# Layer 3 attention: full-width products as four column tiles of 32, and one copy of a pair of transposes on VectorE

## The chip, the cores and the metric

The kernel runs on one core of a Trainium2 chip. The metric is the device time of one execution in microseconds, as the median of three runs. Beside it stands one profiled execution, from which every duration below comes.

## The reference, cut to what matters

The program is a network of four mixed layers on an input of 8 images with 256 channels and 32 x 32 positions, all in 32-bit floats. The change touches only the attention of layer 3. There, every image is 1024 tokens of 256 channels, in 8 heads of 32 channels:

```
qkv = x @ qkv_w.T + qkv_b
scores = einsum('bnhd,bmhd->bhnm', q, k) * scale          # scale = 32 ** -0.5
t = square(scores + 5.0)
attn = t / sum(t, axis=-1)
out = einsum('bhnm,bmhd->bnhd', attn, v) @ proj_w.T + proj_b
```

The input x is the layer-normed state, and the result is added to the state. After it comes a mixture of experts with a router. The denominators have a closed form: the sum over m of (scale q.k + 5) squared needs only the second moments of k per head (a 32 x 32 block) and the sum of k, both independent of the query.

## The kernel before, in words

P is 128, N is 1024 tokens, C is 256 channels, so KC = 2 chunks of 128 channels, HF = 512 is half of the tokens and NT = 8 is the number of token tiles of 128. A chunk of 128 channels holds four heads of 32.

The attention of layer 3 is the generator `fast3`, and its main loop is `attention`. The loop has 256 steps, numbered from 0: 8 images x 2 halves of the queries x 2 chunks x 8 tiles of keys, so 32 steps for an image (image 2 has steps 64 to 95). One step i does, in this order:

- scores (L2745): four matmuls, one for each head of the chunk. A head has 32 channels, so each uses 32 rows of the array and all 128 columns ("32*128" in the profile). They fill two PSUM tiles s from a pool of three.
- squares (L2751): two ScalarE activations of 128 x 1024, giving the tile e of the step. ScalarE works in program order.
- `run(i, beside)`: pieces of other streams that are due at this step: the norm of the image after next (`norm`, on VectorE by L1030 to L1041, plus two short activations), the routing of the image before (`routed`, L2435 is its costliest VectorE line), a fetch, and now and then sorting. What they issue goes to VectorE, ScalarE, GpSimd and the DMA queues.
- a small piece, if one is due and the stream of pieces stands at number 12, 14 or 26 (`SMALL`), so that this step holds two pieces.
- values of step i - 1 (L2725): four matmuls, one for each head, with 128 rows and 32 columns each ("128*32"), accumulated in the single PSUM tile A over 8 key tiles. At the end of such a row VectorE multiplies A by the reciprocal denominators into o (L2730), and A is free again.
- one piece: the output projection of an earlier half (`project`, L2709, two for each half), or else the next piece of the next image's `products`.

The pieces of `products(b + 1)`, 30 for an image, are in order: 8 of k and q (label qk), 4 of v, 4 of kT (two pairs of transposes of k, numbers 12 to 15), 2 of G (moments of k, 129 columns wide, L2668), 4 of Gq (moments times q, L2680), 4 of D (sums over the channels of a head, L2688), then 4 of xn (transposes of the image after that, numbers 26 to 29). All have 128 rows and 128 columns ("128*128"). Each takes the one PSUM bank X and ends with one instruction that empties it: ScalarE for q, k, kT, D and xn, VectorE for v, G, Gq and proj. A D piece gives ScalarE a logarithm (L2689), and every second one an exponential over 1024 columns (L2691).

The profile shows a product of 32-bit floats as two matmul instructions, each with a weight load (PEld); a transpose is one. Matmuls through the helper `linear` all bear line L78, so they are told apart by the tile names. Inside the loop the order on TensorE, VectorE and ScalarE is that in which the code issues the instructions (`net.in_order`); for all else a scheduler arranges them. Before the loop, image 0's products are issued all at once, together with image 1's transposes.

Of the kernel before, what the change touches and what calls it, by code (L numbers as in the profile page):

```python
# [17 lines left out]
P = 128  # L18
B = 8
C = 256  # L20
KC = C // P
N = 1024
HF = 512
# [874 lines left out]
class Fast:  # L898
# [114 lines left out]
    def token_norm_steps(self, dst, x, pool, placed=True):  # L1013

        n = x.shape[1]
        r = pool.tile([P, 2, n], F32, tag="tn_r", name="tn_r")
        yield from self.token_statistics(r, x, pool, placed)
        for t in range(n):
            self.nc.vector.tensor_scalar(
                dst[:, t, :], x[:, t, :], r[:, 0, t : t + 1], r[:, 1, t : t + 1], ALU.mult, ALU.add  # L1020
            )

    def token_norm_pieces(self, dst, x, pool):

# [1532 lines left out]
def fast3(net, io):  # L2557
    tc, nc = net.tc, net.nc
    NH = 4
    NT = N // P  # L2560
    SCALE = 32 ** (-0.5)
    with ExitStack() as ctx, ExitStack() as tok, ExitStack() as att, ExitStack() as bef:
# [10 lines left out]
        wq, wkk, wv = (net.load(wp, f"l3_w{n}", "(k p) o -> p k o", p=P) for n in "qkv")  # L2573
        wo = net.load(wp, "l3_wo", "(k p) o -> p k o", p=P, eng=nc.scalar)
# [5 lines left out]
        heads = net.load(wp, "f3_heads")  # L2580
# [10 lines left out]
        ps = bank("bo")  # L2591
# [10 lines left out]
        xs, xts, xns, qs, ks, vs, rs = ({} for _ in range(7))  # L2602
# [8 lines left out]
        def norm(b):  # L2611
# [8 lines left out]
            yield from net.token_norm_pieces(normed, xs[b], norms)  # L2620
            nc.gpsimd.tensor_tensor(xs[b], xs[b], bo.unsqueeze(1).to_broadcast([P, NT, C]), ALU.add)

        def turned(b, h, c):
            if b not in xns:
                pool, tag = (own["k1"], "xn") if own else (xpool, "x2")
                xns[b] = pool.tile([P, KC, N], F32, tag=tag, name="xn")
            ps = bank("xn")
            for t in range(4):
                nc.tensor.transpose(ps[:, bass.ts(t, P)], xts[b][:, 4 * h + t, bass.ts(c, P)], net.ident)
            nc.scalar.copy(xns[b][:, c, bass.ts(h, HF)], ps)  # L2630

        def projections(b):

            xn = xns.pop(b)
            for d, w, bias, name in ((ks, wkk, bk, "k"), (qs, wq, bq, "q")):
                d[b] = own["two"].tile([P, KC, N], F32, tag=name, name=name)
                for c in range(KC):
                    for h in range(2):
                        ps = bank("qk")
                        net.linear(ps, w, xn, bass.ts(c, P), bass.ts(h, HF))  # L2640
                        nc.scalar.activation(d[b][:, c, bass.ts(h, HF)], ps, AF.Identity, bias=bias(c))
                        yield
            v = vs[b] = own["two"].tile([P, NT, C], F32, tag="v", name="v")
            for t2 in range(0, NT, 2):
                ps = bank("v")
                for i in range(2):
                    net.linear(ps[:, bass.ts(i, C)], xn, wv, bass.ts(t2 + i, P), slice(0, C))
                nc.vector.tensor_copy(v[:, t2 : t2 + 2].rearrange("p t c -> p (t c)"), ps)
                yield

        def denominators(b):

            kt = flat("kt").rearrange("p (t c n) -> p t c n", c=KC, n=P + 4)
            nc.gpsimd.memset(kt[:, :, :, P], 1.0)
            for t2 in range(0, NT, 2):
                ps = bank("kT")
                for i in range(2):
                    for c in range(KC):
                        nc.tensor.transpose(
                            ps[:, i * C + c * P : i * C + (c + 1) * P], ks[b][:, c, bass.ts(t2 + i, P)], net.ident  # L2660
                        )
                nc.scalar.copy(kt[:, t2 : t2 + 2, :, :P], ps.rearrange("p (h c n) -> p h c n", c=KC, n=P))
                yield
            gm = own["k2"].tile([P, KC, P + 4], F32, tag="gm", name="gm")
            for c in range(KC):
                G = bank("G")
                for t in range(NT):
                    nc.tensor.matmul(  # L2668
                        G[:, : P + 1], lhsT=kt[:, t, c, :P], rhs=kt[:, t, c, : P + 1],
                        start=(t == 0), stop=(t == NT - 1),  # L2670
                    )
                nc.vector.tensor_tensor(gm[:, c, : P + 1], G[:, : P + 1], heads[:, 0].to_broadcast([P, P + 1]), ALU.mult)
                yield
            prod = own["k1"].tile([P, KC, N], F32, tag="prod", name="prod")
            r = rs[b] = own["two"].tile([P, KC, N], F32, tag="r", name="r")

            def product(c, h):
                ps = bank("Gq")
                cols = bass.ts(h, HF)
                nc.tensor.matmul(ps, lhsT=gm[:, c, :P], rhs=qs[b][:, c, cols], start=True, stop=True)  # L2680
                nc.vector.scalar_tensor_tensor(
                    prod[:, c, cols], ps, gm[:, c, P : P + 1], qs[b][:, c, cols], ALU.add, ALU.mult
                )

            def weights(c, h):
                ps = bank("D")
                cols = bass.ts(h, HF)
                nc.tensor.matmul(ps, lhsT=heads[:, 0, :P], rhs=prod[:, c, cols], start=True, stop=True)  # L2688
                nc.scalar.activation(r[:, c, cols], ps, AF.Ln, scale=SCALE * SCALE, bias=rest)  # L2689
                if h:  # L2690
                    nc.scalar.activation(r[:, c, :], r[:, c, :], AF.Exp, scale=-1.0)  # L2691
                    nc.sync.dma_start(out=net.sums3[8 * b + 4 * c : 8 * b + 4 * c + 4, :], in_=r[0:P:32, c, :])

            both = [(c, h) for c in range(KC) for h in range(2)]
            for c, h in both:
                product(c, h)
                yield
            for c, h in both:
                weights(c, h)
                yield  # L2700

        def attention(beside, parts):

            steps = [(b, hh, c, kt) for b in range(B) for hh in range(2) for c in range(KC) for kt in range(NT)]
            es, os, accs, projects = {}, {}, {}, []

            def project(b, hh, t2):
                ps = bank("proj")
                for t in range(2):  # L2709
                    net.linear(ps[:, bass.ts(t, C)], os[b], wo, bass.ts(4 * hh + t2 + t, P), slice(0, C))  # L2710
                xh = xs[b][:, 4 * hh + t2 : 4 * hh + t2 + 2].rearrange("p t c -> p (t c)")
                nc.vector.tensor_tensor(xh, ps, xh, ALU.add)

# [20 lines left out]
            def piece():  # L2734
                if next(parts[0][2], "over") == "over":
                    parts.pop(0)
                    if not parts or parts[0][0] > i:
                        return
                    next(parts[0][2])
                parts[0][1] += 1  # L2740

            for i, (b, hh, c, kt) in enumerate(steps):
                ss = [own["S"].tile([P, 2, HF], F32, tag="S", name="s") for _ in range(2)]
                for h in LATEST:
                    nc.tensor.matmul(  # L2745
                        ss[h // 2][:, h % 2], lhsT=ks[b][32 * h : 32 * h + 32, c, bass.ts(kt, P)],
                        rhs=qs[b][32 * h : 32 * h + 32, c, bass.ts(hh, HF)], start=True, stop=True,
                    )
                e = es[i] = own["e"].tile([P, NH, HF], F32, tag="e", name="e")
                for j in range(2):  # L2750
                    anchor[:] = [nc.scalar.activation(e[:, 2 * j : 2 * j + 2], ss[j], AF.Square, scale=SCALE, bias=five)]  # L2751
                run(i, beside)
                turn = bool(projects) and projects[0][0] <= i
                if not turn and parts and parts[0][0] <= i and parts[0][1] in SMALL:
                    piece()
                if i:
                    values(i - 1)
                if projects and projects[0][0] <= i:
                    project(*projects.pop(0)[1:])
                elif parts and parts[0][0] <= i:  # L2760
                    piece()
# [3 lines left out]

        LATEST = (2, 3, 0, 1)
        SMALL = (12, 14, 26)
        STEPS, anchor = 4 * NT, []

        def products(b):  # L2770

# [32 lines left out]
        for _ in projections(0):  # L2804
            pass
# [5 lines left out]
        beside, parts = [], []  # L2811
# [16 lines left out]
        def run(i, streams):  # L2828

            while streams:  # L2830
                d = min(streams, key=lambda d: d[0])
                if d[0] > i:
                    break
                try:
                    next(d[2])
                    d[0] += d[1]
                except StopIteration:
                    streams.remove(d)
# [511 lines left out]
```

## Time and profile before

| what | time |
|---|---|
| median of three runs | 4171.65 us (4161.88 to 4172.53) |
| profiled execution, its own time | 4110.1 us |
| profiled execution, span from first to last instruction | 4108.3 us |
| loop of layer 3's attention within the span | 2804 to 3720 us |
| TensorE busy in the loop | 887.72 of 916.00 us |
| VectorE / ScalarE busy in the loop | 475.25 / 645.24 us |
| a step with scores and values alone, at its shortest | 2.07 us |
| a step with a q or k piece / a v piece | 3.98 / 3.99 us |
| a step with a Gq or D piece / with G | 3.12 / 4.05 us |
| a step with two kT pieces | 4.50 us |

A line of a timeline gives the start in us, the length in us, the engine, the line of the code, the operation, the tiles (out, then in), the part of the array (rows * columns) and the count. The length runs until the last of the merged instructions has ended, so it overlaps the next one. To know what a block costs TensorE, take the difference of two starts. A line of waits gives who waited for whom, the us in total, how often, and the longest.

### The profile page before, as it was taken

Reading aid. Unit: us, or ns where it says so; the run is one execution under the profiler, and the core shown is the slowest. Engines: PE = TensorE matmul, PEld = TensorE weight load, DVE = VectorE, ACT = ScalarE, POOL = GpSimd, SP = SyncE. Lnnn points to the kernel's source line nnn. Section 1 sums busy time; section 2 is a strip of 40 time slices with the busy share of each in tenths; the row PEclk is TensorE's granted clock in tenths of the full one; section 3 lists DMA queues with packets and bytes.
Section 4 is the critical chain, followed back from the end, with each engine's and each line's share of the span. In section 5 each row is a group of like instructions: output and inputs, shape, how many; then the busy total and the mean of one; then the engine's idle time right before and its main releaser. Section 6 shows DMA issues by size and latency. Waiting matters only on the chain. (4 is left out here: it accounts for less than half of the span.)

```text
span 4108.3 us, 52125 instructions
## 1 busy us (share of the span) xinstructions
PE 3745.4 (91%) x19046; PEld 1810.0 (44%) x19046; DVE 2510.4 (61%) x5010; ACT 2306.0 (56%) x3142; POOL 569.1 (14%) x646
## 2 busy tenths in 40 slices
PE   8999999999978788789999978989999999999997
PEld 3323333333334444444444435654333333336886
DVE  2398798798896489952322255852355665467455
ACT  4556566566554377743333445535776766776454
POOL 0000000000000000000000012441000051035753
PEclk9999999999998899989999988999999999999998
DMA  3313223323221577720000012432320041046676
GB/s 102 115 44 111 102 69 115 103 69 106 79 93 55 175 250 291 266 101 11 31 21 21 27 55 90 144 128 65 108 99 25 32 137 50 22 137 192 207 237 218
DMA packets 209947, 442.19 MB, mean 108 GB/s; under 512 B 22025, under 2 KB 132572, under 8 KB 197140
## 3 DMA queue, kind: packets, MB, share of 16 engines
q1 hardware_dynamic: 186580, 387.21, 28.5%
q0 software_dynamic: 19440, 46.45, 3.4%
q10 hardware_dynamic: 3664, 5.11, 0.4%
q8 instruction: 154, 2.52, 0.3%
q14 instruction: 109, 0.89, 0.1%
HBM read 283.34 MB, written 162.28 MB: 108 GB/s over the span
## 5 line engine op out<-in xcount | busy, mean ns | idle before, releaser
L1286 DVE SCALAR_TENSOR_TENSOR a<-hp,w_f_vec,a 128x961 f32<-128x961 f32 (+1 forms) x496 | 608.4, 1232 | 100.0 <-ACT a L1279 91.3
L2751 ACT ACTIVATE e<-s,five 128x1024 f32<-128x1024 f32 x512 | 542.2, 1110 | 217.4 <-PE s L2745 216.2
L2745 PE MATMUL s<-q,k 32*128 32x512 f32 x2048 | 306.1, 641 | 0.0
L1438 ACT ACTIVATE e<-s 128x1024 f32<-128x1024 f32 x256 | 250.2, 1023 | 72.2 <-PE s L1432 61.5
L1392 DVE TENSOR_TENSOR sum<-sum,e 128x1024 f32<-128x1024 f32 x192 | 230.4, 1219 | 86.8 <-ACT e L1438 86.8
L2725 PE MATMUL A<-e,v 128*32 128x512 f32 x2048 | 274.5, 608 | 4.7 <-DVE o L2730 3.4
L1396 PE MATMUL A<-e,va 128*32 128x512 f32 x2048 | 264.1, 615 | 0.0
L2435 DVE SCALAR_TENSOR_TENSOR junk<-mo_x,w_f_wr 128x256 f32<-128x256 f32 x512 | 250.2, 489 | 13.3
L78 PE MATMUL pi<-xn,w_l_wpi 128*128 128x512 f32 x512 | 240.6, 611 | 14.7 <-ACT u L1539 9.2
L1432 PE MATMUL s<-q,k 32*128 32x512 f32 x1024 | 179.9, 649 | 2.5 <-ACT e L1438 2.5
L2950 PE MATMUL h<-xk,w 128*128 128x128 f32 x1192 | 153.8, 284 | 11.6 <-DVE xk L2936 11.5
L1743 PE MATMUL acc<-wt,z 128*64 128x192 f32 (+4 forms) x1344 | 123.5, 326 | 44.2 <-DVE wt L1798 43.9
L1048 POOL DMA_INDIRECT res<-y,to x149 | 149.6, 1004 | 102.7 <-DVE y L2974 41.6
L2919 ACT COPY w<-w_l3f_w 128x512 f32 x149 | 92.4, 626 | 122.0 <-PE h L2950 118.7
L78 PEld LDWEIGHTS pi<-xn,w_l_wpi 128*128 128x128 f32 x512 | 93.8, 193 | 151.0 <-issue 112.5
L2950 PEld LDWEIGHTS h<-xk,w 128*128 128x128 f32 x1192 | 150.8, 200 | 17.6 <-DVE xk L2936 14.0
L1048 POOL DMA_INDIRECT so<-xl,rows x128 | 130.7, 1021 | 192.1 <-issue 151.1
L2745 PEld LDWEIGHTS s<-q,k 32*128 32x128 f32 x2048 | 91.0, 183 | 147.1 <-issue 142.2
L1477 ACT ACTIVATE hp<-pi,pib 128x512 f32<-128x512 f32 x128 | 87.2, 690 | 114.9 <-PE pi L78 114.9
L2970 PE MATMUL y<-w_l3f_w,hid 128*128 x596 | 145.5, 385 | 4.4 <-ACT hid L2956 2.5
L1347 POOL MEMSET thrice<- 32x128 f32 x32 | 6.3, 196 | 1013.8 <-PE pe L1363 1013.7
L1396 PEld LDWEIGHTS A<-e,va 128*32 128x32 f32 x2048 | 58.2, 111 | 174.5 <-issue 173.1
(404 smaller groups left out, 7032.9 us busy)
## 6 DMA issues: line engine op xcount, KB each, us to landing
row<-shifts SPq DMA_DIRECT2D x144, 512.0 KB
x<-d SPq DMA_DIRECT2D x31, 1024.0 KB
xs<-so SPq DMA_DIRECT2D x73, 260.0 KB
so<-zero SPq DMA_DIRECT2D x5, 3380.0 KB
thrice<-vimg SPq DMA_DIRECT2D x64, 256.0 KB
gated<-st SPq DMA_DIRECT2D x32, 512.0 KB
hc<-gated SPq DMA_DIRECT2D x32, 512.0 KB
xl<-mox SPq DMA_DIRECT2D x64, 256.0 KB
```

Of the source, the lines that this page charges most:

```text
L78: self.nc.tensor.matmul(ps, lhsT=w[:, i, m], rhs=src[:, i, cols], start=(i == 0), stop=(i == k - 1))
L1048: made = self.nc.gpsimd.indirect_dma_start(**args)
L1286: nc.vector.scalar_tensor_tensor(to, fr, taps(t_), to, ALU.mult, ALU.add)
L1392: nc.vector.tensor_tensor(half, half, e[j], ALU.add)
L1396: nc.tensor.matmul(state["A"][32 * h : 32 * h + 32, c, :], lhsT=vas[b][:, kt, c, 32 * h : 32 * h + 32], rhs=e[h // 2][:, h % 2, :], start= ...
L1432: nc.tensor.matmul(ss[h // 2][:, h % 2], lhsT=ks[b][32 * h : 32 * h + 32, bass.ts(kt, P)], rhs=qs[b][32 * h : 32 * h + 32, bass.ts(gq, HF) ...
L1438: nc.scalar.activation(es[i][j], ss[j], AF.Exp, scale=SCALE)
L2435: nc.vector.scalar_tensor_tensor(junk, xn[:, t, :], 1.0, self.wr[:, e, :], ALU.mult, ALU.mult, accum_out=pr[:, t, e : e + 1])
L2725: nc.tensor.matmul(A[32 * h : 32 * h + 32], lhsT=vs[b][:, kt, c * P + 32 * h : c * P + 32 * h + 32], rhs=e[:, h, :], start=first, stop=last,)
L2745: nc.tensor.matmul(ss[h // 2][:, h % 2], lhsT=ks[b][32 * h : 32 * h + 32, c, bass.ts(kt, P)], rhs=qs[b][32 * h : 32 * h + 32, c, bass.ts(h ...
L2751: anchor[:] = [nc.scalar.activation(e[:, 2 * j : 2 * j + 2], ss[j], AF.Square, scale=SCALE, bias=five)]
L2950: nc.tensor.matmul(ps[:, j, m], lhsT=ws[j][:, k, bass.ts(m, P)], rhs=xk[:, j, k], start=(k == 0), stop=(k == KC - 1),)
```

## The change

Products with 128 weight columns are issued as four matmuls of 32 columns each: to PSUM partitions 0 to 31, 32 to 63 and so on, all with the same moving operand. That is the form which the values already have. It concerns q, k, v, G, Gq, D and proj, in the loop and before it; the transposes stay as they are. Second, a small piece (the first of two in a step) moves ahead of `run(i, beside)`, and while it is issued the list `quick` is filled, which sends its copy to VectorE instead of ScalarE. The second piece of the step copies on ScalarE as before.

```diff
+    def columns(self, ps, lhsT, rhs, **flags):
+        for h in range(P // 32):
+            self.nc.tensor.matmul(ps[32 * h : 32 * h + 32], lhsT=lhsT[:, 32 * h : 32 * h + 32], rhs=rhs, **flags)
+
+    def linear_columns(self, ps, w, src, m, cols, k=KC):
+        for i in range(k):
+            self.columns(ps, w[:, i, m], src[:, i, cols], start=(i == 0), stop=(i == k - 1))
...
+        def copy(dst, src):
+            (nc.vector.tensor_copy if quick else nc.scalar.copy)(dst, src)
+
...
-            nc.scalar.copy(xns[b][:, c, bass.ts(h, HF)], ps)
+            copy(xns[b][:, c, bass.ts(h, HF)], ps)
...
-                        net.linear(ps, w, xn, bass.ts(c, P), bass.ts(h, HF))
+                        net.linear_columns(ps, w, xn, bass.ts(c, P), bass.ts(h, HF))
...
-                    net.linear(ps[:, bass.ts(i, C)], xn, wv, bass.ts(t2 + i, P), slice(0, C))
+                    net.linear_columns(ps[:, bass.ts(i, C)], xn, wv, bass.ts(t2 + i, P), slice(0, C))
...
-                nc.scalar.copy(kt[:, t2 : t2 + 2, :, :P], ps.rearrange("p (h c n) -> p h c n", c=KC, n=P))
+                copy(kt[:, t2 : t2 + 2, :, :P], ps.rearrange("p (h c n) -> p h c n", c=KC, n=P))
...
-                    nc.tensor.matmul(
-                        G[:, : P + 1], lhsT=kt[:, t, c, :P], rhs=kt[:, t, c, : P + 1],
-                        start=(t == 0), stop=(t == NT - 1),
+                    net.columns(
+                        G[:, : P + 1], kt[:, t, c, :P], kt[:, t, c, : P + 1], start=(t == 0), stop=(t == NT - 1)
                     )
...
-                nc.tensor.matmul(ps, lhsT=gm[:, c, :P], rhs=qs[b][:, c, cols], start=True, stop=True)
+                net.columns(ps, gm[:, c, :P], qs[b][:, c, cols], start=True, stop=True)
...
-                nc.tensor.matmul(ps, lhsT=heads[:, 0, :P], rhs=prod[:, c, cols], start=True, stop=True)
+                net.columns(ps, heads[:, 0, :P], prod[:, c, cols], start=True, stop=True)
...
-                    net.linear(ps[:, bass.ts(t, C)], os[b], wo, bass.ts(4 * hh + t2 + t, P), slice(0, C))
+                    net.linear_columns(ps[:, bass.ts(t, C)], os[b], wo, bass.ts(4 * hh + t2 + t, P), slice(0, C))
...
-                run(i, beside)
                 turn = bool(projects) and projects[0][0] <= i
                 if not turn and parts and parts[0][0] <= i and parts[0][1] in SMALL:
+                    quick.append(i)
                     piece()
+                    quick.clear()
+                run(i, beside)
                 if i:
                     values(i - 1)
...
-        STEPS, anchor = 4 * NT, []
+        STEPS, anchor, quick = 4 * NT, [], []
```

## The prediction

> **What bounds the kernel now.** I read the busy shares first, then the busy time by stage, then the timeline of single steps, then TensorE's waits in the stage that the change touches.
>
> ```profile
> PE 3745.4 (91%) x19046; PEld 1810.0 (44%) x19046; DVE 2510.4 (61%) x5010; ACT 2306.0 (56%) x3142; POOL 569.1 (14%) x646
> ```
> ```profile
> 2804.00:3720.00 916.00, 887.72 (x5351) 321.33 (x5349) 475.25 (x1702) 645.24 (x699) 167.06 (x159) 1.00 0.24 76
> ```
> The second line (stage and its length; busy PE, PEld, DVE, ACT, POOL; clock; DMA) is the loop of layer 3's attention: PE is busy 887.72 of 916 us, DVE half, ACT 70%. So PE's own work is the bound there; but "busy" holds gaps between instructions, and those the timeline shows.
>
> ```profile
> 3040.30 1.14 PE L2745 MATMUL s<-q,k 32*128 32x512 f32 x8
> 3041.37 1.07 PE L2725 MATMUL A<-e,v 128*32 128x512 f32 x8
> 3042.37 1.13 PE L2745 MATMUL s<-q,k 32*128 32x512 f32 x6
> ```
> ```profile
> 3082.55 1.14 PE L2745 MATMUL s<-q,k 32*128 32x512 f32 x8
> 3083.62 1.07 PE L2725 MATMUL A<-e,v 128*32 128x512 f32 x8
> 3084.62 1.99 PE L78 MATMUL v<-w_l_wv,xn 128*128 128x256 f32 x8
> 3086.54 1.14 PE L2745 MATMUL s<-q,k 32*128 32x512 f32 x8
> ```
> ```profile
> 145.15 1.92 PE L1396 MATMUL A<-e,va 128*32 128x512 f32 x16
> 147.00 0.70 PE L1432 MATMUL s<-q,k 32*128 32x512 f32 x2
> ```
> Read differences of starts. Scores take 1.07, values 1.00 to the next start; the v piece takes 1.92 for 8 full-width instructions. Steady full-width work of that shape ran 47 instructions in 10.31 us (y, L2248); less the last one's 0.38 that is 9.93 / 46 = 0.216 each, and 8 x 0.216 = 1.73. The other 0.19 to 0.20 is paid for entering and leaving a full-width block. The q/k piece says the same: 1.92 for four, while h (L78) ran 15 in 6.60 us, (6.60 - 0.59) / 14 = 0.43 each, 1.72. Layer 0 has column tiles in a row: 16 instructions, four rounds of four tiles, take 1.85 to the next start; two rounds take 1.00 above. A further round of four column tiles thus costs 0.43, what one full-width instruction over the same 512 columns costs.
>
> The stalls are at pairs of transposes:
>
> ```profile
> 3099.59 0.66 PE L2659 MATMUL kT<-ident,k 128*128 128x128 f32 x4
> 3101.79 0.59 ACT L2662 COPY kt<-kT 128x512 f32<-128x512 f32 x1
> 3102.43 0.66 PE L2659 MATMUL kT<-ident,k 128*128 128x128 f32 x4 [1.19 <-ACT kt L2662]
> ...
> 3105.81 0.69 DVE L2730 TENSOR_TENSOR o<-A,r 128x512 f32<-128x512 f32 x1
> ```
> ```profile
> PE kT L2659 <- ACT kt L2662: 16.7, 14, 1.2
> PE xn L2629 <- ACT xn L2630: 5.3, 6, 1.7
> PE A L2725 <- DVE o L2730: 3.4, 1, 3.4
> ```
> The second four need the one X bank; the copy that frees it stands behind 2.12 us of squares on ACT. The last line is a warning: the A bank is single too, and once its reader was late on DVE.
>
> [...] The groups show 108 ns (A) against 189 to 190 (v), 81 less. [...] its densest stretch, 46 instructions of L1743 in 3.41 us, is 74 ns per matmul with its load.
>
> **The change, part by part.** Sums are against the profiled execution (span 4108.3, time 4110.1); the runs' median of 4171.65 is 61.6 above it. No view shows where those lie, so I carry the saving over in us.
>
> *1. Column tiles.* Behind values in the same mode a piece loses the 0.20 and keeps its rounds: the q/k step goes from 3.98 to 3.78, the v step from 3.99 to 3.79. By the groups' counts the loop has 56 q/k pieces (224 instructions / 4), 28 v and 30 proj (/ 8), 28 Gq and 28 D (/ 2), 14 G (/ 16). For G, 15 in 1.84 us are (1.84 - 0.28) / 14 = 0.112 each; its 1.98 against 16 x 0.112 = 1.79 leaves 0.19. D apart (part 2), I count all but the 2 proj of the last image whose steps wait on ACT or DVE: 154 x 0.199 = 30.6 us.
> Unknown: rounds of 256 and 129 columns in column tiles are in no row. Their tiles stream the same columns, so I take the full-width pace, 0.216 and 0.112. [...] the worse end is issue: TensorE's instructions per piece rise fourfold (rival 3). Before the loop the same pieces stand between transposes, with no switch now and about 9 after: 9 x 0.13 = 1.2 lost.
>
> *2. Sums (D).* ACT then has per two steps 4 squares in 4.24, two logarithms of 0.6 and an exponential of 1.0, together 6.4, against PE's new 2 x 2.92 = 5.85. Now e ends 0.25 us before its values at the worst step. Followed by hand from image 2's step 89 (squares 1.27 behind their scores; ln 0.6, exp 1.0 in program order): the fourth D step waits 0.27, the bank behind it 0.22 more. The transposes that follow (at 3150.69) now go ahead of the route's two counting products, which need X and wait 0.9 for the new copy; in return the second four lose their 0.72. The five steps shrink from 17.56 to about 16.8: 0.76 for each of images 1 to 5, 3.8. Image 0 has no route, its 1.72 stall goes, and with it the half clock that followed (scores 1.86, values 1.94 at 2907.54): by the same sum 3.6. The block before the last image, ACT-bound behind D, 0.4. Together 7.8.
>
> *3. First kT copy on DVE.* 14 times 4.50 us; without a stall 2.07 + 2 x 0.59 = 3.25. Transposes begin 1.07 into a step, the copy can start 0.70 later and lasts 0.69 (v's row), ending at 2.46, ahead of the second four at 2.65. So the named stall goes. What is late next is DVE. In images 1 to 5 these two steps hold 4.16 and 4.26 us of DVE (windows), nearly all their time. New DVE chain from step 79's start: v copy to 0.72, idle until 1.77 for the transposes, copy to 2.38, 2.82 of route and norm to 5.20, copy to 5.81, 3.76 of route and norm to 9.57, o to 10.26. PE reaches the next accumulator at 3.25 + 3.28 + 1.07 = 7.6 and waits 2.7 for o to free A; today it starts there at 3108.59 - 3098.51 = 10.08. The stall moves from X to A: +0.2 each. Behind the waiting DVE copy stand the route's and norm's pieces and o; behind A, proj. Besides, long pauses were followed by a clock of 0.50 (after 1.72 and 3.38 us idle), which costs some 1.6 us (0.72 on scores and 0.88 on values at 2907.54); I take it 3 times in 5. So 5 x 0.2 + 3 x 1.6 = 5.8 lost. Image 0's steps have 0.69 and 0.00 of DVE: 2 x 1.25 = 2.5 won. The sixth (4.12 and 2.44): o ends at 8.3, 1.65 won. Sum of part 3: -1.6. ACT's relief by 0.59 a copy is worth nothing where it is idle anyway. Moved ahead along with the first kT is POOL's fill of the ones column (0.13 us); the piece issues no DMA, and nothing on SP changes place.
>
> *Elsewhere.* The built order differs in the expert stage too, where last-image route pieces come at other places; no wait there names them: 0, with 5 either way.
>
> Sum: 30.6 - 1.2 + 7.8 - 1.6 = 35.6, about 36 us; 4110 to 4074 in the profile, **4171.65 - 36 = 4136 us** for the runs.
>
> **The rivals.**
> 1. *The stalls go whole*: DVE catches up, no wait on A. For it: DVE is idle in the steps ahead (0.00 at step 75). Against: the chain above. Adds 5.8 plus 5 x 2.5: 54 saved, 4118.
> 2. *Small narrow rounds are slower*: v, proj and G keep only half of their saving or pay 0.02 per round: 72 x 0.2 lost, 14; 22 saved, 4150. With all of it eaten by ACT and DVE, 4172.
> 3. *Issue becomes PE's bound, and the kernel slower.* Place: a v step has 16 + 16 + 64 = 96 loads and matmuls in 3.79 us, 39 ns each; a G step 160 in 3.85, 24 ns. Today's G pays 0.112 for a load and a matmul, 56 each. [...] Against: L1743 did 37 ns per instruction for 3.4 us[...].
> 4. *The tiles don't overlap* is excluded by layer 0's rows for 512 columns.
>
> **How the numbers follow.** Forecast (4124 to 4147) 0.62; rival 1 0.13; rival 2 0.10; no change 0.07; rival 3 0.08. A measurement of this kernel tells about 0.3%, 12.5 us, from no change: faster is below 4159, 0.84; same 0.08; slower 0.08. Range: from 4113 (rival 1 with 5 us more) to 4158 (rival 2 with 8 less).
>
> **What would show it.** Right: q/k and v steps of 3.78 to 3.79; rounds of 0.43, 0.216 and 0.112; kT's wait on ACT gone; PE A waiting on DVE o, 2.7 us five times; D's fourth step longer than 2.92. Wrong: v or G rounds stretched, with weight loads idle for "issue" (rival 3); no wait on o (rival 1); a clock below 1.00 in the loop.

## The result, and the profile after

| | runs, median (lowest to highest) | profiled execution |
|---|---|---|
| before | 4172.09 us (4153.7 to 4185.73, 6 runs) | 4110.1 us, span 4108.3 |
| after | 4132.33 us (4125.82 to 4139.9, 6 runs) | 4139.9 us, span 4138.1 |

The ratio of the runs is 0.991 (95% interval 0.9883 to 0.9936): faster by 40 us. The profiled executions say the opposite: the kernel before ran at 4111 to 4113 us in three sets of runs (like its profile) and at 4160 to 4172 in two (like the profile of after), one of the chips showing both, so times are compared only within a set, and profiles only stretch by stretch. The after kernel measured once more beside a before of 4111.06 took 4079.81 (ratio 0.9919, 0.99 to 0.9937), and that profile, called *after again*, is the one to hold against that of before.

First the page's line of engine totals, of after. Against before (19046 matmul instructions) it has 22502, yet TensorE's busy time hardly moved (3745.4 us in before): the narrow instructions run four side by side, their starts 7 ns apart.

```profile
PE 3755.4 (91%) x22502; PEld 1791.9 (43%) x22502; DVE 2522.3 (61%) x5030; ACT 2296.6 (55%) x3122; POOL 571.5 (14%) x646
```

The loop of layer 3 in after again, by stage (stretch and length; busy PE, PEld, DVE, ACT, POOL; clock; DMA). It lasts 875.9 us; the same view of before, from the first to the last step's start, lasts 911.8. So the loop gave 36.0 us. The part behind it went from 391.6 to 392.6; the loop's start, 2804.9 us in before, lies anywhere between 2802 and 2824 us in the other profiles of the sets of 4111 to 4113, 2818.8 here.

```profile
2818.80:3694.70 875.90, 852.76 (x8410) 291.63 (x8406) 487.16 (x1719) 631.49 (x676) 165.97 (x157) 0.99 0.25 80
```

Single steps in the timeline of after again: a v step, then a G block.

```profile
3091.15 1.14 PE L2757 MATMUL s<-q,k 32*128 32x512 f32 x8
...
3092.22 1.06 PE L2737 MATMUL A<-e,v 128*32 128x512 f32 x8
...
3093.11 1.91 PE L1026 MATMUL v<-w_l_wv,xn 128*32 128x256 f32 x32
...
3094.95 1.14 PE L2757 MATMUL s<-q,k 32*128 32x512 f32 x8
...
3115.45 1.94 PE L1026 MATMUL G<-kt 128*32 128x129 f32 x64
3117.32 1.14 PE L2757 MATMUL s<-q,k 32*128 32x512 f32 x8
```

Starts again: the v step takes 3.80 (3091.15 to 3094.95) where it took 3.99. Values to v is 0.89 instead of 1.00, and v to the next scores 1.84 instead of 1.92. The weight loads (PEld) show where the two parts come from. First before, then after again:

```profile
3084.62 1.59 PEld L78 LDWEIGHTS v<-w_l_wv,xn 128*128 128x128 f32 x8 [0.84 <-issue]
```
```profile
3092.68 0.13 PEld L1026 LDWEIGHTS v<-w_l_wv,xn 128*32 128x32 f32 x4 [0.30 <-issue]
...
3093.11 1.43 PEld L1026 LDWEIGHTS v<-w_l_wv,xn 128*32 128x32 f32 x28 [0.30 <-issue]
```

In before the first load of v starts 0.54 us behind the second round of the values (at 3084.08), and the first v matmul takes 0.32 to the next instead of 0.216. In after again the first four loads of v start together with the second round of the values (3092.68), and the first round of v follows 0.43 behind it, which is the bare pace of rounds. So both parts of the price lie at the entry: 0.11 us of standing between the two shapes, and 0.10 for a first load that nothing covers (together 0.20, as the four tiles of a round start 7 ns apart and so end 0.02 later). The way out costs the same in both: from the last v instruction to the next scores 0.31. G's 64 matmuls with their loads take 1.87 us.

The pair of transposes in after again (image 2), and what came late next:

```profile
3096.02 0.66 PE L2672 MATMUL kT<-ident,k 128*128 128x128 f32 x4
...
3096.71 0.69 DVE L2634 COPY kt<-kT 128x512 f32<-128x512 f32 x1 [0.92 <-PE kT L2672]
...
3097.60 0.66 PE L2672 MATMUL kT<-ident,k 128*128 128x128 f32 x4
...
3104.48 0.66 DVE L2742 TENSOR_TENSOR o<-A,r 128x512 f32<-128x512 f32 x1
...
3105.29 1.74 PE L2737 MATMUL A<-e,v 128*32 128x512 f32 x8 [2.69 <-DVE o L2742]
3106.72 3.05 PE L1026 MATMUL proj<-w_l_wo,o 128*32 128x256 f32 x32
```

The second four start 1.58 us after the first and wait for nothing (before: 2.84, of which 1.19 was the wait). But two steps on, A waits 2.69 us for o, and what follows runs slowly: values 1.43 to the next start, proj 2.98 instead of 1.84. The stage view gives a granted clock of 0.62 for that stretch (3105.2 to 3109.7), and 0.50 in the middle of it (3106 to 3108). Such a stretch is called a half clock below. TensorE's waits in the loop of after again (us in total, times, longest):

```profile
PE A L2737 <- DVE o L2742: 14.9, 8, 3.5
PE mo_n L2493 <- DVE xn L2634: 3.9, 5, 0.8
PE kT L2672 <- DVE kt L2634: 2.7, 3, 0.9
```

In before these were 16.7 us of kT waiting for ScalarE, 5.3 of xn and 3.4 of A. (mo_n are the two counting products of the routing.)

The first profile of after has a loop of 887.3 us. Images 0 to 3, 5 and 6 are within 0.12 us of after again; images 4 and 7 are 5.1 and 6.4 longer, because single instructions start late there. In image 4, ScalarE and then TensorE:

```profile
3311.22 0.69 ACT L2654 ACTIVATE k<-qk,w_l_vec 128x512 f32<-128x512 f32 x1 [2.93 <-PE s L2757]
```
```profile
3311.96 1.92 PE L1026 MATMUL qk<-xn,w_l_wk 128*32 128x512 f32 x16 [1.21 <-ACT k L2654]
```

The qk that this instruction reads was finished by 3308.7, and ScalarE had nothing else to do until 3311.22. Images 4 and 7 are late in the profiles of the three experiments of the set of 4160.26 too, and in no other. Why is not known.

### The profile page after: what moved, and what is told of

It is laid out like the page before. It is cut to its first block, busy times and chain, and to the rows that moved or that the text cites. A ratio compares the mean times of both kernels' runs of the same rounds, so it can differ in the third digit from the quotient of the medians.

```text
span 4138.1 us, 59047 instructions
## 1 busy us (share of the span) xinstructions
PE 3755.4 (91%) x22502; PEld 1791.9 (43%) x22502; DVE 2522.3 (61%) x5030; ACT 2296.6 (55%) x3122; POOL 571.5 (14%) x646
## 5 line engine op out<-in xcount | busy, mean ns | idle before, releaser
L2258 PE MATMUL y<-w_l2f_w,hid 128*128 128x256 f32 x512 | 126.5, 402 | 17.4 <-issue 17.2
```

## The experiments

The loop is from the first to the last step's start; the ratio is to the kernel before in the same set (median of that set in brackets).

| kernel | loop, us | runs, us | ratio (95%) |
|---|---|---|---|
| columns only (set of 4110.81) | 882.4 | 4081.23 | 0.993 (0.9913 to 0.9947) |
| copy only | 910.2 | 4109.01 | 1.0001 (0.9989 to 1.0014) |
| two tiles of 64 | 896.6 | 4101.81 | 0.9975 (0.9964 to 0.9986) |
| o first | 861.4 | 4061.79 | 0.9886 (0.9867 to 0.9906) |
| after again (set of 4111.06) | 875.9 | 4079.81 | 0.9919 (0.99 to 0.9937) |
| sums (D) wide | 879.2 | 4082.07 | 0.9925 (0.9907 to 0.9942) |
| norm later | 871.5 | 4077.86 | 0.992 (0.9903 to 0.9937) |
| o first, norm later | 860.8 | 4065.91 | 0.9885 (0.9865 to 0.9904) |
| norm later, add held (set of 4160.26) | 876.1 | 4128.45 | 0.9932 (0.9916 to 0.9949) |
| o first, norm later, add held | 865.1 | 4121.91 | 0.991 (0.9893 to 0.9927) |
| o first, copies on ScalarE | 905.5 | 4156.27 | 0.9991 (0.9978 to 1.0004) |
| o first, norm later, add held, again (set of 4113.26) | 856.0 | 4056.96 | 0.9881 (0.9855 to 0.9907) |

The runs of one set differ by 20 us and more, so the steps are told apart by images. Change of each image of 32 steps against the profile of before, in us (image 7 to its last step's start):

| kernel | 0 | 1 | 2 | 3 | 4 | 5 | 6 | 7 |
|---|---|---|---|---|---|---|---|---|
| after again | -10.15 | -4.77 | -3.03 | -3.03 | -4.18 | -4.73 | -6.29 | +0.21 |
| columns only | -4.04 | -4.48 | -4.42 | -4.42 | -3.84 | -4.43 | -4.43 | +0.68 |
| copy only | -5.91 | +1.51 | +1.52 | +1.52 | -0.11 | +1.52 | -1.85 | +0.18 |
| two tiles of 64 | -7.06 | -1.40 | +0.23 | -1.39 | -1.31 | -1.39 | -2.96 | +0.02 |
| sums (D) wide | -9.76 | -2.74 | -2.68 | -2.67 | -3.82 | -4.37 | -6.07 | -0.56 |
| o first | -10.14 | -6.60 | -6.34 | -6.33 | -6.01 | -6.60 | -7.11 | -1.34 |
| norm later | -10.15 | -4.03 | -4.68 | -3.10 | -6.78 | -5.57 | -6.29 | +0.23 |
| norm later, add held | -10.15 | -6.87 | -5.94 | -5.94 | +0.63 | -6.83 | -6.28 | +5.62 |
| o first, norm later | -10.15 | -6.94 | -6.19 | -5.86 | -8.04 | -5.38 | -7.11 | -1.41 |
| o first, norm later, add held, again | -10.15 | -8.05 | -7.28 | -7.26 | -6.19 | -8.05 | -7.11 | -1.73 |
| o first, copies on ScalarE | -4.10 | -1.91 | -0.21 | -1.49 | +3.50 | -1.96 | -4.58 | +4.38 |

**Columns alone, and the copy alone.** Each half of the change, put on the kernel before. The first keeps every product of the diff as column tiles and takes out `copy`, `quick` and the moved `run`; the second is the reverse.

> Column tiles as in the change, but both copies of a pair on ScalarE and the small piece behind run(i, beside), as before. My theory[...]: q/k steps 3.78, v 3.79, Gq and D 2.92, G 3.83 us as in the changed kernel; kT steps stay at 4.50 with about 17 us of waits for ScalarE; waits on o in images 1 to 5 go (the A bank is free long before). Loop 911.8 - 31 - 3 = about 878 us, that is the changed kernel's loop or a little less, and some 34 us less than before in the runs. Rival (the gain comes from the copies and the column tiles only fill gaps): loop above 895 us.

> The first copy of a pair on VectorE and the small piece ahead of run(i, beside), with full-width products as before. My theory (the stall only moves from X to A where VectorE is full): kT steps fall from 4.50 to about 3.25 to 3.3 us in all images, but values behind them wait about 2.7 us for o in images 1 to 5, 0.7 in image 6 and nothing in image 0, partly with a half clock after it; loop 912 - 2.5 (kT, image 0) - 1.6 (image 6) - 3.5 (xn, image 0) - 1 + 1 to 6 = 903 to 911 us; the runs within 0.3% of before. Rival (the whole wait of 22 us on ScalarE is won): loop 890 us, the runs 20 us faster.

Columns alone save 29.4 us of the loop and 29.6 of the runs, some 4 less than expected. Of that, 1.8 lie in the step with the transposes and mo_n, which grew from 5.07 to 5.43 us in five images: most of what the narrow D wins ahead of it is lost there. The copy alone saves 1.6 of the loop, as expected, and nothing in the runs. TensorE's waits with columns alone, then with the copy alone:

```profile
PE kT L2669 <- ACT kt L2672: 16.7, 14, 1.2
PE xn L2639 <- ACT xn L2640: 5.8, 6, 1.9
```
```profile
PE A L2728 <- DVE o L2733: 14.7, 7, 3.4
```

The copy takes 16.7 us of waiting at kT and 5.3 at xn away, and sets up 11.3 more at A (14.7 where before had 3.4), 3.9 at mo_n and 2.7 at kT, besides the half clocks. Together the halves give 36.0, 5 more than their sum (881 us had been expected of after again on that sum, 875.9 came). With the copy alone, four of images 1 to 5 fall to the half clock behind A's wait (steps of 7.2 to 8.4 us), in after again only images 2 and 3 (8.25). The two in images 1 and 5 are 3.6 of the 5 us, and they look like chance, for A waits 1.76 or 1.77 us there in both kernels. Images 4 and 5 of the copy alone:

```profile
3350.96 1.06 PE L2728 MATMUL A<-e,v 128*32 128x512 f32 x8 [1.76 <-DVE o L2733]
```
```profile
3469.70 1.90 PE L2728 MATMUL A<-e,v 128*32 128x512 f32 x8 [1.76 <-DVE o L2733]
```

The first values run at full clock, the second at half, after the same 1.76 us. In all this, "the copy" means the engine and the piece's place ahead of `run`; no run parts the two.

**Is it the change of shape, or the narrower load?** The shape is the part of the array in a line of the timeline; the recorded texts call it the mode. The changed kernel with two tiles of 64 columns: not the form of the values, but still with less to load.

```diff
-        for h in range(P // 32):
-            self.nc.tensor.matmul(ps[32 * h : 32 * h + 32], lhsT=lhsT[:, 32 * h : 32 * h + 32], rhs=rhs, **flags)
+        for h in range(P // 64):
+            self.nc.tensor.matmul(ps[64 * h : 64 * h + 64], lhsT=lhsT[:, 64 * h : 64 * h + 64], rhs=rhs, **flags)
```

> The changed kernel with two tiles of 64 columns instead of four of 32. My theory (what is saved is the change of tiling mode behind the values, which a third mode doesn't save[...]): [...] q/k steps about 3.90 to 3.95, v 3.91 to 3.96, D 3.04 to 3.09 us; loop 154 x 0.13 to 0.16 = 20 to 25 us longer than the changed kernel's, before ACT's share. Rival (smaller loads or parallel tiles themselves are what saves): q/k steps at or below 3.83 us, loop within 8 us of the changed kernel's.

The q/k step takes 3.934 us, v 3.944, Gq and D 3.076, G 3.978: 0.15 of the 0.20 comes back, as expected, and the loop is 20.7 us longer. Beside the lines of the v step above:

```profile
3079.93 1.49 PEld L1026 LDWEIGHTS v<-w_l_wv,xn 128*64 128x64 f32 x16 [0.84 <-issue]
```

The first load stands 0.54 us behind the values' second round (3079.39), as with full width: the 0.11 is paid in full. The first round then takes 0.27 to the next, where full width took 0.32 and a bare round takes 0.216: 0.05 of uncovered load instead of 0.10. In before a weight load of 32 columns takes 108 ns on average (A), one of 64 columns 146 (L1743) and one of 128 columns 189 (v). So the two parts are told apart: the change of shape is 0.11 of the 0.20, the uncovered load the rest, and only the very tiles of the values save both.

**What the narrow D gives.**

```diff
-                net.columns(ps, heads[:, 0, :P], prod[:, c, cols], start=True, stop=True)
+                nc.tensor.matmul(ps, lhsT=heads[:, 0, :P], rhs=prod[:, c, cols], start=True, stop=True)
```

> The changed kernel with D (28 pieces) at full width again. By the prediction D's narrow form gains less than 28 x 0.20 = 5.6 us, since ScalarE is nearly full in these steps: the fourth D step waits 0.25 us in six images. So the loop grows by 28 x 0.20 less 6 x 0.25, about 4 us, D steps are 3.12 us all, and nothing else in an image moves. Rival A (ScalarE sets the pace there): D's narrow form gave nothing, the four D steps and the transposes behind them take the same time together, and the loop is within 1 us of the changed kernel. Rival B: it gave all of 5.6 us.

The loop grew by 3.3 us. Of that, 1.7 is a half clock in image 1 (its step 49 takes 7.32 us instead of 5.63) that after again did not have, and image 7 is 0.8 shorter. Elsewhere the narrow D gives 0.35 to 0.36 us an image (2 to 5), 0.39 in image 0 and 0.22 in image 6: 2.4 in all, if image 1 has its 0.36. The four D steps give 4 x 0.20 less 0.25, as expected; but the step behind them, with the transposes and mo_n, takes 4.87 us in after again and 4.68 here. That 0.19 was missed: the answer lies between "about 4" and rival A. The half clock in image 1 came after a wait of A of 1.77 us, as long as in after again, so nothing ties it to D.

**Why o is late.** Two ways to shorten VectorE's queue ahead of o. The first moves the other pieces behind the values, so that o is queued ahead of them; the second starts the norm two steps later.

```diff
-                run(i, beside)
                 if i:
                     values(i - 1)
+                run(i, beside)
```

> The changed kernel with one line moved: run(i, beside) behind values(i - 1), so that VectorE gets o ahead of the step's pieces of routing and norm, and TensorE gets the routing's two counting products behind the values. My theory (values wait on o, which stands behind up to 3.8 us of VectorE work; mo_n waits 0.9 for the copy): the waits of A on o in images 1 to 6 fall from 2.7 to under 0.5 each, those of mo_n on xn from 4.0 us to nearly none; VectorE is still full in these steps, so up to 1.5 us an image comes back as a wait of proj on x; loop 5 to 15 us shorter than the changed kernel's. Rival (VectorE's total is the bound there, its order is nothing): the wait comes back in full at proj, loop the same within 3 us.

```diff
-                beside.append([at + 15, 1, norm(b + 2)])
+                beside.append([at + (17 if b else 15), 1, norm(b + 2)])
```

> The changed kernel, with the norm of the image after next started two steps later in images 1 to 5, so that its 1.08 us a step of VectorE leave the two steps with kT. My theory (VectorE's queue ahead of o is what makes A wait): o ends 2 x 1.08 = 2.2 us earlier, A waits about 0.5 instead of 2.7 us in images 1 to 5, the half clock behind that wait goes, and the kernel is 5 x 2.2 to 5 x 3.8, 11 to 19 us faster than the changed kernel. Rival (the copies alone, or the route, make o late; or the wait moves to the proj step that now carries the norm's piece): A still waits 2 us or more, or proj waits for x as long, and the time is within 5 us of the changed kernel.

O first holds: the waits of its loop are

```profile
PE proj L1026 <- DVE x L2724: 4.7, 6, 1.5
...
PE A L2737 <- DVE o L2742: 2.6, 1, 2.6
```

and the loop is 14.5 us shorter than in after again: a wait of A for o of 1.8 to 2.7 us, in some images with the half clock behind it, has become one of proj for x of at most 1.5. In five images 0.4 us more comes from the step with mo_n (4.47 us instead of 4.87), where mo_n now stands behind the values and doesn't wait. Norm later gave only 4.4 in the loop and nothing in the runs. A's wait shrank from 1.76 to 0.6 in images 1, 4 and 5, about as expected, but in images 2 and 3 only from 2.69 to 1.50: with less ahead of it, VectorE reached the second copy early and stood 0.80 us waiting for the transposes, in order. And a new wait came, mo_n for xn, 9.0 us instead of 3.9. The timeline of VectorE and GpSimd (norm later) shows its cause:

```profile
3123.79 0.19 DVE L2476 TENSOR_SCALAR chosen<-rank 128x64 f32<-128x64 f32 x1
3124.02 0.23 DVE L2478 TENSOR_TENSOR tmp<-chosen,pr 128x64 f32<-128x64 f32 x1
3124.28 0.22 DVE L2479 TENSOR_REDUCE weigh<-tmp 128x8 f32<-128x64 f32 x1
3124.41 4.33 DVE L2476 TENSOR_SCALAR chosen<-rank 128x64 f32<-128x64 f32 x1
```
```profile
3124.01 4.68 POOL L2631 TENSOR_TENSOR x<-x,w_f_bo 128x2048 f32<-128x2048 f32 x1 [66.72 <-DVE chosen L2476]
```

The same instruction takes 0.19 us, and 4.33 when GpSimd's add has begun before it; both end within 0.05 us of each other. The add is the norm's last piece; two steps earlier, in after again, it had lain on nothing that it held (chosen took 205 ns on average). Why it holds this instruction the traces don't show; tmp and weigh, which started after it too, took 0.23 and 0.22 us. The next kernels hold the add (it waits for the squares of the image's last step).

```diff
+            late = own and b > 2
+            for _ in range(4 if late else 0):
+                yield
-            nc.gpsimd.tensor_tensor(xs[b], xs[b], bo.unsqueeze(1).to_broadcast([P, NT, C]), ALU.add)
+            add = nc.gpsimd.tensor_tensor(xs[b], xs[b], bo.unsqueeze(1).to_broadcast([P, NT, C]), ALU.add)
+            if late:
+                net.wait_for(add.ins, [a.ins for a in anchor])
```

> As e5_norm_later, with the norm's last instruction, GpSimd's add of 128 x 2048 (4.6 us), held until the squares of the last step of the image (it waits for them). In e5_norm_later that add came to lie on the route's instruction chosen (L2476) on VectorE, which took 4.33 us there instead of 0.19 and ended with the add. My theory: VectorE was held by GpSimd, and that alone took e5's gain. Then chosen takes 0.2 us in all images, mo_n waits 4 us in all instead of 9, A waits for o as in e5 (9.2 us), and the loop is 5 x 1.26 us and the half clock shorter: about 864 us against 871.5 in e5_norm_later and 875.9 in the changed kernel; the runs 12 us below the changed kernel. Rival: the long chosen had another cause, and the wait stays: 871 us.

Chosen took 205 ns on average again, so it was the add that held it; mo_n's wait fell to 3.1 and A's is 9.8. Images 1, 2, 3 and 5 are 2.1 to 2.9 us shorter than in after again; 12 for the five, as expected, if image 4 did likewise. It can't be read in images 4 and 7, which are late in this set, and the runs (0.9932) don't show the gain; only the images do.

**The pieces together.**

> The kernel with o ahead of the other pieces (e3_o_first), with the norm started two steps later as well. What was left there at the two kT steps was a wait of proj for x, up to 1.5 us in images 1 to 5, behind the same VectorE queue. If the queue is the cause, 2.2 us less of it takes that wait away: about 5 us less than e3_o_first, 4057 where that had 4062. Rival: the norm's pieces land in the proj steps and delay them by as much: no difference from e3_o_first.

> As e6_o_first_norm_later, with the same hold on GpSimd's add. In e6 the add lay on the route's instructions in four images; image 4, where it did not, was 8.0 us shorter than in the kernel before, the others 5.4 to 6.9. If the hold removes this, images 1 to 5 are all about 8 us shorter: a loop of about 853 us against 861, and the runs 6 to 8 us below e3_o_first's 4062. Rival: the hold delays the sort that stands behind the add on GpSimd, and the expert stage gives it back: loop 853, runs as e3_o_first.

> The same kernel as e9_o_first_add_later once more. In its first measurement the kernel before took 4160 us instead of the 4111 beside which e3_o_first was measured, and the profile had late starts in images 4 and 7. My theory: these go with the executions near 4160, not with the kernel. Where the kernel before takes about 4111 again, image 4 is 8 us shorter than before, like images 1 and 5, the loop is about 853 us against 861 in e3_o_first, and the runs are about 4055, a ratio of 0.986 to 0.987. Rival: the held add delays the sort behind it on GpSimd and the experts: the loop is 853, but the part after it grows, and the ratio is 0.9886, that of e3_o_first, or worse. If the kernel before takes 4160 again, image 4 has its late starts again and this stays open.

With o first and the norm later, but the add not held, no gain came: proj's wait fell from 4.7 to 2.0, and the add lay on the route in four of five images (mo_n waits 4.4). With the add held, images 1 to 3 and 5 gain 7.3 to 8.1 us each, twice. The loop, measured where nothing else is late, is 856.0, not 853: in image 4 a proj still waits 1.64 us for x (its step takes 5.64), in images 2 and 3 one waits 0.6. The part behind the loop is 394.7 against 392.2 with o first alone. At 4056.96 (0.9881) it is the fastest kernel here. Its loop is 19.8 us shorter than the changed kernel's, but in the runs even those two intervals (0.9855 to 0.9907 and 0.99 to 0.9937) touch; against o first alone they overlap.

**Does o first need the copy?** O first with every copy on ScalarE.

```diff
-                    quick.append(i)
                     piece()
```

> e3_o_first with every copy on ScalarE again (columns, o ahead of the other pieces, no copy on VectorE). My theory: o first is worth nothing by itself, as the copy was worth nothing by itself; only together do they free the kT steps. Then this kernel is the columns-only one: kT steps 4.50 us, a wait of kT on ScalarE's copy of 16.7 us, a loop of about 882 us, runs about 20 us above e3_o_first. Rival: o first is worth its gain without the copy, since in the kernels with the copy it took away waits of A: then the loop is 870 us or less.

Both theories were wrong. kT's 17.3 us of waiting on ScalarE are back, as expected, but there is a loss besides: 2.5 to 4.2 us for each of images 1, 2, 3 and 5 against columns alone, and no gain over the kernel before.

```profile
PE kT L2672 <- ACT kt L2634: 17.3, 14, 1.8
PE mo_n L2493 <- ACT xn L2634: 9.6, 5, 1.9
```

mo_n needs the bank X behind the first transposes of xn, whose copy stands behind two squares on ScalarE; that step takes 6.5 to 6.9 us, and behind it the clock halves (scores take 2.09 us instead of 1.14). On top of the columns, then, the copy is worth 6.6 us of the loop (882.4 to 875.9) and hardly anything in the runs, o first alone costs 2.5 to 4.2 us an image, and the two together are worth 21.0.

## Why the prediction was right

*Column tiles, 154 x 0.199 = 30.6.* Right in mechanism and size. q/k 3.783 (3.78 forecast), v 3.793 (3.79), Gq and D 2.925 (2.92), G 3.827 (3.85). The unknown, rounds of 256 and 129 columns, takes the full-width pace: 0.216 for v and 110 ns a round in G, 0.112 forecast. One reading was wrong: the 0.20 isn't paid "for entering and leaving" a full-width block. It all lies at the entry, 0.11 for the change of shape and 0.10 for the first load, which the two-tile kernel tells apart.

*Ahead of the loop, -1.2.* Right, though the 0.13 a switch was an estimate of the author. There the products stand between transposes. From the first kT to the first D it takes 10.77 us in before and with the copy alone, 11.56 in after and after again; from the last xn to the first qk 0.91 and 1.05. That is 0.93 lost, where 1.2 was forecast, and the 0.79 of the first stretch for its 7 changes of shape is 0.11 each, uncovered loads included.

*Sums, 7.8.* The fourth D step takes 3.17 (forecast 2.92 and 0.25), mo_n waits 0.8 five times (0.9 forecast), and the five steps take 3 x 2.925 + 3.171 + 4.867 = 16.81 us, forecast 16.8. What the text did not say is how that divides: of the 0.75 an image, the narrow D brings 0.36, the transposes that go ahead on the quick copy the rest.

*The copy, -1.6.* Right in mechanism: the stall moved from X to A. o ends 10.19 us after step 79's start (10.26), A waits 2.69 (2.7), the half clock costs 1.69 (1.6): images 2 and 3 take 3.265 + 8.248 for the second kT step and the proj step, images 1, 4 and 5 4.19 + 5.63. It came in two of five images, not three, and that it was not one or four is luck: the same waits brought four with the copy alone, three with D wide and one with two tiles. Images 1, 4 and 5 pay a wait of 0.9 at the second four instead and only 1.8 at A, which the chain worked out from image 2 did not foresee. All that the sum credits to the copy, here and under D (5 x 0.39 and image 0's 3.6), is 4.0; after again is 6.6 below columns alone. The term was too small by the third half clock (1.6) and 1 us more.

By image, the terms of the sum give 10.1 for image 0 (20 x 0.199 + 3.6 + 2.5), 4.9 or, with the half clock, 3.3 for images 1 to 5, 6.4 for image 6 and 0.4 for image 7. After again shows 10.15; 4.77, 3.03, 3.03, 4.18, 4.73; 6.29; -0.21. Sum 36.8 for the loop, measured 36.0; with one half clock more or less it would be off by 1.6.

*The 61.6 us* between profile and median were carried over without a reason. The two profiles of after show where such a difference lies: in the first the loop begins at 2843 us instead of 2819, images 4 and 7 are 5.1 and 6.4 longer, and the part behind the loop takes 408 instead of 393. The saving came out as 40 us beside the one before and 31 beside the other, and the intervals of the ratio (0.9883 to 0.9936 and 0.99 to 0.9937) overlap: that the first lies so near the forecast 36 is in part luck. What makes single instructions start late stays open.

*The signs.* All those of "right" came: steps and rounds, no wait of kT on ScalarE, a fourth D step of 3.17; only A's wait on o was 2.7 twice and 1.8 three times. Of the signs of "wrong" one came as well, a clock below 1.00 in the loop (0.99, and 0.62 behind A's wait). It was a poor sign, since part 3 counted on three half clocks.

*The rivals.* Stalls gone whole (1): no, but o first shows that this was to be had. Narrow rounds slower (2): no. Issue (3): no. G's 128 loads and matmuls in 1.87 us are 14.6 ns each; how many of them had been issued ahead the trace doesn't show. Ahead of the loop in after again, from the first v to the third xn behind it, 280 matmuls and as many loads ran without a wait in 13.80 us (2796.70 to 2810.50), 25 ns each; in the first profile of after it was 559 instructions in 14.64 us, 26 each. With none issued ahead, a pace of about 40 ns would have eaten the gain, by an estimate from the measured steps of an image: four v steps of 96 instructions and two G steps of 160 are 704, and they would have to take 4 x 3.793 + 2 x 3.827 + 36.0 / 7 = 28.0 us. That TensorE would issue at 56 ns was an estimate of the author from the 0.112 us of a load and a matmul of G in before, and no trace here shows it for the narrow form.

## What to carry to other kernels

A full-width block behind column tiles of 32 cost TensorE 0.20 us here, whether it had 2, 4 or 8 instructions (0.22 with 16): 0.11 for the change of shape and the rest for a first weight load that nothing covers. Give short products the shape of what runs just ahead of them, and their first loads can go under its last round, as those of v did here (3092.68). A copy moved to an idle engine is worth what the next queue leaves of it (here, alone, 1.6 us of the loop, of 22.0 waited for ScalarE); look at what stands there ahead of the instruction that frees the next buffer, and put that one first. Before moving a piece, see where its instructions on other engines come to lie (GpSimd's add stretched an instruction of 0.19 us to 4.33).

## What was not expected of the hardware

- GpSimd's add of 128 x 2048 held a VectorE instruction of 0.19 us for 4.33. Not every one is held: beside the same add prod took its usual 0.75 us (after again), and tmp and weigh 0.23 and 0.22 (norm later).
- Two tiles of 64 columns behind four of 32 pay 0.15 us of the 0.20 that a full-width block pays: the change of shape in full, half of the uncovered load.
- TensorE ran 64 matmuls with their loads, 128 instructions, in 1.87 us, and 560 in 13.80 (after again; 559 in 14.64 in the first profile of after).
- The length of a wait doesn't settle whether the clock halves. In the loops of all these profiles it halved after each wait of 3.38 us and more. Below that both happened: halved after 1.72 (before) and 1.76 us (copy alone, image 5), once even after 1.02 followed by 0.38 (o first, norm later, image 5); not halved after 1.76 (copy alone, image 4), 2.67 (o first, copies on ScalarE) and 2.69 (two tiles, image 3).
